# Another order table, and other planned costs, for a four-layer graph-attention kernel

## The chip, the cores and the metric

The kernel runs on one core of one Trainium2 chip. The metric is the device time of one execution in microseconds; the figure for a version is the median of several executions. A core has five engines, each with an instruction queue of its own that it works through strictly in program order: PE (matrix products), DVE (vector), ACT (activations), POOL (general, here small vector work and the issue of accumulating transfers) and SP (issue of plain transfers). The engines wait for each other by semaphores, which the tool chain sets from the data that instructions share. An instruction that has to wait therefore holds up everything behind it in its own queue, also work that could already run.

## What is computed

Sixteen independent graphs (a batch of 16, 1024 nodes, 256 features) pass four layers; all share one 1024 x 1024 adjacency matrix. Before each layer there is a layer norm and a ReLU, and each layer's result is added to its input.

```python
h = jnp.maximum(_layernorm(x, axis=-1), 0.0)
x = x + _L0_gnn_ref(h, adj, L0_gnn_W, L0_gnn_a)      # one-head graph attention, relu
h = jnp.maximum(_layernorm(x, axis=-1), 0.0)
x = x + _L1_gnn_ref(h, adj, L1_gnn_W, L1_gnn_a)      # one-head graph attention, elu
h = jnp.maximum(_layernorm(x, axis=-1), 0.0)
x = x + _L2_gnn_ref(h, adj, ...)                     # 8-head dot attention, norm, feed-forward, norm
h = jnp.maximum(_layernorm(x, axis=-1), 0.0)
x = x + _L3_gnn_ref(h, adj, L3_gnn_W, L3_gnn_a)      # four-head graph attention, elu
```

In a graph-attention layer the weight of node j for node i is the softmax over j of leaky_relu(e_i + e_j) where the adjacency is set. In layer 2 it is the softmax of q k / sqrt(32) where it is set, head by head.

## The kernel before

The work is cut into **stages**, one for each layer and graph (64 of them), and stages of up to four graphs are interleaved. All of it is written down first as 12,154 small operations (`op(...)`): for each an engine, a cost in us, the operations that it comes after, and the buffers that it takes and ends. One operation is a handful of instructions, for example four matrix products.

`play()` then lays the operations out. It calls `forward(rank)`, a list scheduler that keeps a clock for each engine, adds each operation's cost to it, and adds `DELAY[engine]` before a result counts as seen elsewhere. At every step it looks at the operations that could start on an engine, takes those that could start within 0.5 us (`SLACK`) of the earliest, and picks the one of lowest rank. Changes of PE's tile shape are charged by `SWITCH`. The ranks come from a long string, `RANKS`, with three characters for each operation; since it has the right length, it is used and no other ranks are tried. The order in which operations are picked is the order in which instructions are emitted on every engine's queue. So both the string and the costs decide the order, and neither is in the program that runs: they cost no instruction.

The operations that the prediction speaks of, with their lines in the profile:

- **Layers 0 and 1**: eight weight blocks on DVE (p, L1362), then the products `av` on PE (L1379, eight operations of four products for each half of the nodes), whose result in one of two PSUM banks is inverted on DVE (L1396), taken out by ACT (L1402, L1417) and added on DVE (L1407, L1421, L1422).
- **Layer 2**: `scores` on PE (sc, L1597; four heads), two exponentials on ACT (L1611), two mask products on DVE (L1619), `values` on PE (acc, L1628). For each pair of such items a 1,024 KB transfer that adds one tile to the other (pe<-pe) is issued on POOL (L1645), and `totals` on PE (sums, L1658) uses the result. At the end of a half: a copy on ACT (L1668), transposes on PE (L1677), normalisation, feed-forward products `up` and `down` (both L1097), between them a transfer that adds an offset row to y (y<-offsets, issued on POOL, L1733) and another to x. Then DVE adds (L1797), ACT squares the result (L1071), POOL takes the root (L1074, L1075), DVE scales and adds (L1812, L1819).
- **Layer 3**: weight blocks on DVE (L1443) after a transfer of source values (r<-kept, SP), `values` on PE (acc, L1477) and `totals` (sums, L1501).
- **The way into each layer**: squares or statistics, a root, a normalisation on ACT or DVE (L1151, L1135, L1144), eight transposes on PE (tp, L1090), a copy on ACT (hT, L1093), then products (pm, L1097).

A second path through the file, for inputs that break the fast path's assumptions, is compiled and not run here.

PE works with three tile shapes: the whole array, 32 rows by 128 columns (scores) and 128 rows by 32 columns (acc and sums of layers 2 and 3).

Of the kernel before, what the change touches and what calls it, by code (L numbers as in the profile page):

```python
# [28 lines left out]
U8 = mybir.dt.uint8  # L29
# [3 lines left out]
AX = mybir.AxisListType  # L33
PSUM = bass.MemoryType.PSUM

P = 128
# [11 lines left out]
    "$7K#`;$57#};#U[#8d#-f##%###$'v#;a#.U##$#$5#$&$6j#Pq#$(#cE##E#$W#$<#xV##=#%#$Jw#$;##,#$H#$o#+$#Jm#$w#+d##+#%?$1;"  # L48
    "#H)#&R#')#'C#'O#'.#':#'R#'b##f#+###3##r$=O##I##j#*}##H##v#*b#Tz#cL#`U##0##6##C#$I#$G#$T#Gf#$7##5#$F#iA#$_##-#%)"
    "##y#ok##F##|##G##h#$'#`@#*-#$-#*i#`R#S$#WI#$}#%U##4#%x#$[#$Z##z#$E#$i#$2#%p#we#$O#%t#*j#*`#$A##&#$C#)>$&R$<_#vY"  # L50
    "$<6#JZ#%V#)u#)2#$K#(K#(-#wg#%h#&4#&%#&]##x#$Q##u##.#%l#%z#$@##P#$|#''#$a#-m#$]#]<#'?#%:#$D$BL#$j#]:#%7#&Y$H;#&8"
    "#%D$19#$:#AB#%u#&?#}=#&S#%9#%_#',#&A#'-#&q#v_#$P##Y#&B#%i#&w#'g#&`#'7#%n#'I#_p#L=#b##$h#$p##L#$u#$q#$y#%%#$L##W"
    "#%-#%W#%<#%`#'a#'6#&(#%3#%d#&t#cA#%J#&H#A:##R#%[#%k##9#'U#%s##`#,L#'&##S#%g#$4#'`#%B#%v$#8##c#%f#&z#c:#$e$Iu#Xf"
    "$*R#&9#%}#Xg#&:#_/$-O#uE#%G#*g#EY#T8#ui#$c$CA$H8#$n#3%#Tp#%F#2b#%@#${$Ew#&C##b#%M#$f#$0#%H#$z#$%#%/#$l#%4#$M#%N"
    "#%8#%e##(#&I#%+#t<#j?#%,$.f#&M#%.#2?#]0##n#'E#$v#%$#$t#$m#%m#%^#'j#(m#'H#(d#$x#&*#&[#&o#%q##J#']#-@#%P#%1#'Q#vX"
    "#EX#:B#$.#%I##7#$d#%a##_##8#$3#'W#'{#&'#/r#%=#az$KE#$b#'4#L`#$$#b$#0:#_0$*r#R9#$##&m#+q#*$#09#&u$*q$Kt#&1#'>#05"
    "$7h#R8#%0##a#0F#[F#'T#&i#$J#G>#&e#_g#ov#(,#GS#(}$:)#&K#%r#&^#%A#&n#&&#%&#$B$8R#&v$Ks#&j$LG#Fy#'%#JJ#&/#)P#&$$(M"
    "#&p$08#uH#tF#o7#)O#&F#%o#%b#&+#*(##X$9B#&>#%O$9##'|$9Y#DY#$>#'P#'_#'l#(5#)@#'}#?+#%6#(6#Y.#[N#[M#<R#0j#(##%2#q_"
    "#qN$9n#*M##K#&c#&b#'=#$R#1Q##Z##2#o4#$*#($#$?#(/#%R$9p#oM#&V#I8#-2#DZ#Kr#1d#,B#&G#'9#Jq#*q#$8$9v$:_#y7#6?#'f#K="
    "#(s#r:#(r#'*$Bb#_s$%L#([#JM#(<#AL#(I#w_#r5#&E#&P#(%#,_#(*#VI$+d#'c#'q#KL#.-#(f#-V$4l$Je#'r#((#;3#H+#<&#)#$?&#AO"  # L60
    "#ck#(8#&O#vO#83$5F$:^$7.#(.#(C#&g#(J#&=#(R#)K#(V#(l#(U#)0#)%#)|#)D#)S#+2#;7#%w#&a#$)#'1#&_#%*#$`#(7#(X#%y#(y#i*"
    "#&h#u,#re#(_#(W$0=$23$0<#&U$FK#&T#(L#(2#K##(D$/n#)r#0n#(A#(v#(N$0;#)q#(0#)p#0m$8Y#)3#)-#Gq#4f#)x#)E$$A#=Q#G]#'L"
    "#i+#H8#'d$3a#Jy#()#)/#)8#'t#)b#(a$8u#vv##B#)1#)9#D,#)g#,q##A#vo##@#)6#)Y#)7$Ho#)+#QW#uq#),#(@#)d#'F#$N#)*$=##)C"
    "#+k#*:#*s#,g#-r#+0#71#0t#0(#(|#q<#D4#pz#D:#*>#)R$6w#(e#QZ#D(#,.#)G#`-#*T#*9#*a#.j#,1#*B#*H#*l#Dk#LC#*'#-j#*W#'["
    "#u4#*Q#*4#{s#-h#D3#9J#*_#*J#p|#B##La#.8#*v$5.#7I#+4#*[#eE#.D$IK#*u#*U#*S#)h#.>#(P#.<#*X$;}#+B#=B#+R#*h#nE$+q#(O"
    "##]#*f#*]$5?$Ij$M.#+m#+>$5%#u3#+Q#+<$L]#>x#Ig#+l#*V#+=#/'#[p$B@#<;#+^$-|#Y_#+Y#*%$B?#zG#XR#K{#+L#+&#+c$O%#+j#<_"
    "#+i$4}$<>#+u#*y#)_#y($Ai#}A#+g#+]$C,$6m#Wb#L%#,,#M=#aC#{a#+5#rn#,>#C/#+`#+[$Ek#?>#*8#,f$0H##D#)4#)T#*K#+|#jE#+%"
    "#&X#,n$G;#,'#(G#..#e2#+b$7r#?k#Qu#)L#g9#*m#on#nl#.Z#+-#=R#Jt#.'#.]#-x#.H$E4#H@#-U#-a#/_#.G#.P#0.#-]#l;#*x#/V#/L"
    "$(9#.O$OJ$Dr#.I#/f##<#0B#.N#^T#/9#.*#-W#.r#.9#1)#0<#/U#.S$A:#D1#fV#;2#/3#.;#+,#+*$<H#y)#Va$9G#+f#,/$Ah#*<#LD$7-"
    "#,*#VV#T&#,9#-+$?)$Bc#M<#C'#{>#)W#rY#Cn$:i#Cm#,C$-{#T%#,o#,7#/,$7D#4e#+C#,^#,6#/.#+a$:h#)}#,v#aB#['#,V#+M#&W#,N"  # L70
    "#0g#?R#-Q#,d#.,#,;#+)#?Q#-O#0-#(F$Oa#+O#+.#(h#,}#*P#,u$Dz#-$#.0#,Z#l4#-&#,D#+9$7;#-?#,j#(g#-%#]s#,0$/$#+w#m:#,h"
    "#]e#,8#-=$?3#RV#0D#-N#nI$Mt$7v##*$G=#-y#,a#.V#Ht#/4#,M#(`#p9$(y#.J#l<#+1#,W#:a#/b#,e#om#*7#-q#*R#+H$Do#*w#1+#+G"
    "#/z#,l#-u#,z#,|#.R#.$#-(#*/$>o#.a#oP#.:#--#/%#+K#-B#/>#._#-X#.^#o,#.b#.v#Qz#BC#mJ#QP#0h#`=#-G$J{$Kv#(M#&s$5D#.A"
    "#&r#0$#)m#1P#,y$J0#1Z#0+#&-#-w#be#,{#/}#*O#/k#-A#&)#,U#/g#,(#+z#/5#0)#h0#,`#-p#,r#'2#,X#.C#g0#/t#0k#u$#0/#/{#-^"
    "#+_#.{#/6#/K#/Y#/X#1&#*e#.B$,_#]3#_(#oN#(b#0l#VS#)`#)^#*Z#*&#,?$0z#+/#+h#,k#*t#*,#*G#**#*L#(3#8+$8;#*)#+($59$J|"
    "#WB$.g$J_#yG#+e#)n#+:#-;#)o#+3#-e#,O#LX$0E#2J#+D#*A#I3#*z#dg#.=#s,#s-#.w$/X#+E#,J#*C#+7#/+$'I#Tk#A-#)l#+o$6d$#`"
    "#,x#|=#)B#-S#-_#-I#-|#-}#-v#)?#/l#+}##?#0U#S:#^S#0X#2M$(x#-8#.t#.h#9|#-R#mG#ff#.d$CJ#(H#/H#:.#t##/0#/($B;$)K#/#"
    "#[?$=C#[a#-K#/[#.K#.u$7m#,Q$5H#,G#mt#/v#,F#3D$5G#jF$KK$>T#.p#2D#od##>#S;#2E$CI#.q#q^#Kz#.7#0>#//#.E#EF#Sr#0*#hd"
    "#tv#f?#P0#-*#0E#0C#/8#,&#/^#mu$=<#-t#0?#2Y#l&#/J$<;#mA#{f#/o#Ci#-M#8`#1J#3,#29#`D#0L#if#ie#pF#0G#;p#{H#8k#/)#]?"
    "#_<#[z#+;#+Z#+T#+{#30#1*#1i#,R#+N#+U#Do#1;#./#ol#q}#/y#H&#31#qH#-o#)Z#.4#Gk#}x#4K#/T#Yz#0`#0K#15#.[#2o#1j#0H#.&"  # L80
    "$J3#/x#0]#,##+J#/P#/Q$'V#0r#0Z#0z#1?#1$#1F#1R#0[#1/#0f#/$#11#1>#03#5.#1E#1:#2m#1[$N-#1o#0o#@-#(Y#5<#);#b4#1(#aA"
    "#1z#6]#7Y#/1#-c#1Y#^6$JQ#1e#/7#12#1C#Se#2*$;s#@1#H^$*{#0x#-b#0p#9y#1k#?b#/]#1y#(Z#1f$BO$-i#e-#tJ#2&#/&#cO#0S#5;"
    "#1g$1/#2=$Hh#1h#bj#0b$-h$*T$*(#2B$*6$+|#0|$JU#2)#1=$*4#{*#2T$K7#2X#2(#1^#@.#M%#2O#/e#/m#5'#p{#2^#0%#/d#4E#7e$K6"
    "#53#2G$+T$>W#21#1n#/Z#S)#-k#A+#0^#1B#-1#T.#nV#6W#2[#>%$@p#2Z#2'$Iw#58#1`#[-#1s#2C#,t#]b$Iv#,:#4O#46#M'#26#/?#nW"
    "#(k#pq#2$#2:#2Q#oX#^v$$m#.1#3/#Hk#>$$>V#0M#>B#1m#3;#.F#2A#3C#3>#2_#3M#4D#3T#/G#3Q#42#3U$-]#3N#8n#3v#9f#3P#8j#5q"
    "#?I#44#)i#6t##[#2@#`<#4]#(?$1m#5`#4J#*N#4T#33#OG#*Y#7.#:*#,K#50#L1$C4#t'#U+#*E#R*#7)#1D#zf#zI$-u#1I#/A#8.#5X$Cp"
    "#3B#wq#/E#kJ#37#3i#2|$26#4;#7U#35#7^#:>#59$;,#5x#4x#7=#7L#3L#1q#B9#[w#qy$5Z#2h#2N#oL#WY#OF#[v#43$Bg#4s#3##1x#B'"
    "#o6#D7#,5#2d#2f#mK$'$#K,$#o#3.#3t$?6#1|#07#Ju$OZ#?P#3K#^<#2e#bA#32#mM$'G$EU#3[#4r#2z#25#b_#3A$-?#3R#HV#23#1T#3G"
    "$=J#2W#2##+@#3s#L9#4>#3+$M,#3W#2n#3e#2y#3?$*f#3Z$+R#3]#e5#47#$,#5a#3'#-i#34#+?#1l#3^#17#9S#3f#3<#3u#3w$Mg##l#TB"
    "#2x$1Q#3x#4j#41#4&#2w#J6#4-$7G#4I#40#3g#3@#4Z#3m#70#F|$4s#GO#4<#4,$;Q#B>#7/#6O#4|#BQ#4m#<C#uo$Ld#5_$C8#4?#1<#4N"  # L90
    "#24#3d#4P$.*#5C#6s#3=#4l#5Q$8E#5>#80#3O#-F#69#4k#3}#-E#5O#Be$I|#'D$5/#^V#3S#s`#2l#5h#94#1G#76$?T#5W$Ec#7N#1p#5L"
    "#5y#Bm#By#9W#9k#$1#Br#1,#6a#Bl#5V$Eg#6v##o#7?#6w#f@#Av##e#uz#/i#3|#0J#0O$O$#0T#1t#5s#0P#7##2F#V3#0R#Mm$IW#2{#61"
    "#[4#2]#[0$?H$?A$?R#Bs#F{#6(#6P#6'#zP#Mz#6&#4Q#4=#4C#4y$03#7@#(x#4U#oZ#3($A-#5]#1S#l##4B#tj$+P#T2#5%#51$;Y#60#4F"
    "#X%#s@#5)#5B#36#4:$60#Y=#5o#49#5b#1W$1h#nw#5{#9##78#X9#aw#4%#6j#5z#6n#R,$FF#Qw#5H#5S#7R#2R#fi#6|$6$#r0#5R#5j#Bf"
    "$7+#4##7m#77$IX#5n#6-#6z#7(#7A#W=#6b#}t#6Y#75#hw#W2#hv#yy#7$##^#6Q$Bi#Nj#Vr#o5$*x#Dd$3z#5/#5,#4{#5i#0Y#F7#62#5$"
    "#3*#.T#7z#8O#6d#3c#-s#.W#6i#6u#5##5^#.s#.6#6Z#XQ#6m#6x#r)#7B#O:#7u#2S#79#8U#7i#:?#{N#9O#9h#%K#7g#7V#@9#nv#7|#%]"
    "#8G#7[#6^#8;#85#7k#8-#8S#8D#8B#7v#68#9,#M;$9,#TE#8b#?a#8a#;##8H#9&$>)#<q#8J#_q#Lm$'3#HE#,$#7C#2p$4.#7'#k8#nm#7D"
    "##'#Y0#7G#5v#Em#8R$JF#8&#5g#3V#6o#6{#7%#8N#6D#7a#7t#7P#7K#4^#6G#7T#6;$)%#Y@$El#4w#7-#k`#7d#7x#:8$JE#4*#4v#7J$Kh"
    "#9$#l=#5U#8X$1j#7;#7+#7{#4t#3I#4i#:;#SW#G(#45#4h#@]#@[#Ks#:x#9H#;x#9'#x-#x]#;w#:v$<7#7_#Z&#87#d1$@?#g+#d6#6`#8'"
    "#:P#nX#'e#mW$F<#<6#8s#9Z#<p$>-#-4#86$Eh#<)#6N#98#cl#-g#cq#Ln#Ft#;r#9B#0I#9l#8F#9=#9:#:r#:)#9i#9%#2.#2-$N}#5k#74"  # L100
    "#'m#'z#_M#8E#:o#9?#9M$ER#K7$/m#5[#@W$0,#9D#9[#cp#8e$Ej#/R#F.$,u#9g#9A#&k#:l$,t#<##@_#G&#/D$({#'<#;}#xH#9Y#?p#';"
    "#9R#:I#9d#2r#:s#6K#Ab#8K#&2#:H#8u#;o#I>#x'#9Q#:t#93$#a$#n#8P$/p#;V#mX$+G$B0#95#7p#;U$=h$HX#9E#Fe#;s#:e#9z#9<$IZ"
    "#Cj$3S#84#:4#:9#xo#:(#yc#9{#@^#[A#:y#9K#&3#IB#8w#x.#:`##;#8v#I@#7M#um#:k#cB#Z,#;5#9}$16$,Z#QY#=$#;M#6e#Qb#ns$K-"
    "$,Y#:d#8$$Ki#dk#;=#9>#:=#J:#89#?'#9t#6)#:<#jC#9;#em#;@$DX#<A#;C#9u#:c#4[#;N#el#;1#6I#<8#4n$DP#:}#;k#AX#uT#;P#5J"
# [515 lines left out]
def fast_path(tc, bad, x, adj, l0_w, l0_a, l1_w, l1_a, w_qkv, ln1_g, ln1_b, ln2_g, ln2_b, w1, b1, w2, b2, l3_w, l3_a, out):  # L620
# [13 lines left out]
    with ctx:  # L634
# [128 lines left out]

        ops = []
        PE, DVE, ACT, POOL, SP, QUEUE = range(6)

        DELAY = (0.2, 0.12, 0.14, 0.06, 2.0, 1.4)
        ITSELF = 0.04  # L770

        SWITCH = {None: 0.2, 132: 0.21, 32: 0.125}


        BEFORE_END = 0.1
# [1268 lines left out]
```

## Time and profile before

| what | value |
|---|---|
| median of 3 runs | 4212.4 us (4209.66 to 4214.54) |
| the profiled execution's own time | 4213.85 us |
| its span | 4212.1 us |
| PE busy | 4093.9 us, 97% |
| DVE busy | 3170.0 us, 75% |
| ACT busy | 2322.9 us, 55% |
| POOL busy | 1169.6 us, 28% |
| DMA queue q0 (the POOL-issued transfers) | 302.01 MB, 36.5% of 16 engines' span |
| granted PE clock | 0.994 of full speed |

The profiled execution took 1.4 us more than the median; its span is 1.8 us shorter than its own time. A group line names source line, engine, operation, output and input tiles, then busy time, the mean of one, and the engine's idle time before it with what ended it. A busy PE in this profile can contain waits, because the ends of overlapping products are modelled; the starts are recorded.

### The profile page before, as it was taken

How to read it: one execution, taken by the hardware profiler on the slowest of the kernel's cores; microseconds unless marked ns; L12 is line 12 of the kernel's file. 1: busy time of each engine (PE TensorE's matmuls, PEld its weight loads, DVE VectorE, ACT ScalarE, POOL GpSimd, SP SyncE). 2: the span in 40 equal slices, each digit the busy share in tenths (PEclk: the TensorE clock that was granted, in tenths of full speed). 3: DMA queues.
4: the chain of work that ended last, by engine and by line, in shares of the span. 5: the costliest groups of instructions: out<-in, count | busy, mean ns of one | idle time of the engine just before them, and what ended most of it. 6: DMA issues, size and time to landing. Idle time of an engine off the chain costs nothing.

```text
span 4212.1 us, 67534 instructions
## 1 busy us (share of the span) xinstructions
PE 4093.9 (97%) x25993; PEld 2160.5 (51%) x25993; DVE 3170.0 (75%) x5964; ACT 2322.9 (55%) x4235; POOL 1169.6 (28%) x2025
## 2 busy tenths in 40 slices
PE   8999999999999999999999999999999999999997
PEld 7735255553555536455364654546545465564433
DVE  7577867778677786777867778776787877859697
ACT  5564645636456364564646646465463745666452
POOL 2322231412314123141331423223132241423131
PEclk9999999999999999999999999999999999999999
DMA  3171814518145181451815518164271733636361
GB/s 124 34 158 35 176 45 96 111 49 170 39 99 107 51 170 36 112 108 37 170 38 116 113 35 162 41 135 91 53 151 33 159 67 79 121 82 132 72 135 47
DMA packets 106826, 398.96 MB, mean 95 GB/s; under 512 B 11528, under 2 KB 47744, under 8 KB 73728
## 3 DMA queue, kind: packets, MB, share of 16 engines
q0 software_dynamic: 46080, 302.01, 36.5%
q1 hardware_dynamic: 60000, 92.03, 6.7%
q8 instruction: 206, 3.38, 0.3%
q14 instruction: 124, 1.02, 0.1%
q10 hardware_dynamic: 416, 0.52, 0.0%
HBM read 107.87 MB, written 18.21 MB: 30 GB/s over the span
## 4 chain that ended last, share of the span: by engine, by line
PE 74%; DMA 7%; DVE 6%; issue 6%; ACT 4%; POOL 2%; SPq 0%; POOLq 0%; ACTq 0%; DVEq 0%
PE pm L1097 19%; PE av L1379 18%; PE acc L1477 10%; PE sc L1597 8%; PE acc L1628 6%; DMA pe<-pe 5%; PE sums L1501 5%; PE sums L1658 3%; PE tp L1090 3%; DVE pe L1619 2%; DMA y<-offsets 2%; ACT pe L1611 1%; DVE y L1797 1%; ACT pm L1071 1%; PE tpv L1540 1%
## 5 line engine op out<-in xcount | busy, mean ns | idle before, releaser
L1619 DVE TENSOR_TENSOR pe<-pe,mask 128x1024 f32<-128x1024 f32 x1024 | 1200.6, 1219 | 208.7 <-ACT pe L1611 205.1
L1611 ACT ACTIVATE pe<-sc 128x1024 f32<-128x1024 f32 x1024 | 998.0, 1022 | 321.0 <-PE sc L1597 228.0
L1379 PE MATMUL av<-v,p 128*128 128x257 f32 x4096 | 956.7, 384 | 21.7 <-ACT o L1402 10.7
L1379 PEld LDWEIGHTS av<-v,p 128*128 128x128 f32 x4096 | 764.9, 191 | 210.9 <-issue 60.8
L1443 DVE SCALAR_TENSOR_TENSOR p<-r,e,mask 128x1024 f32<-128x1024 f32 x512 | 623.0, 1274 | 114.6 <-DMA r<-kept 98.0
L1597 PE MATMUL sc<-qT,kT 32*128 32x512 f32 x4096 | 620.9, 642 | 2.7 <-ACT pe L1611 1.5
L1628 PE MATMUL acc<-pe,v 128*32 128x512 f32 x4096 | 538.3, 604 | 1.3 <-DVE pe L1619 0.6
L1645 POOL DMA_DIRECT2D pe<-pe x256 | 224.7, 878 | 992.5 <-PE acc L1628 628.7
L1074 POOL TENSOR_SCALAR rstd<-stats 128x1 f32<-128x1 f32 x512 | 159.0, 311 | 1153.4 <-ACT xn L1071 739.8
L1477 PE MATMUL acc<-p,v 128*32 128x512 f32 x4096 | 463.0, 593 | 0.0
L1597 PEld LDWEIGHTS sc<-qT,kT 32*128 32x128 f32 x4096 | 189.8, 183 | 379.4 <-issue 174.7
L1097 PE MATMUL pm<-l_wx,hT 128*128 128x259 f32 (+1 forms) x1536 | 369.5, 389 | 8.1 <-ACT hT L1093 5.2
L1362 DVE SCALAR_TENSOR_TENSOR p<-r,e,mask 128x512 f32<-128x512 f32 x512 | 349.1, 743 | 24.8 <-DMA r<-kept 19.1
L1075 POOL TENSOR_TENSOR rstd<-rstd,minus_half 128x1 f32<-128x1 f32 x512 | 331.6, 648 | 42.7
L1097 PEld LDWEIGHTS pm<-l_wx,hT 128*128 128x128 f32 x1536 | 287.4, 191 | 79.1 <-ACT hT L1093 20.7
L1658 PE MATMUL sums<-pe,pick 128*32 128x512 f32 x2048 | 269.5, 603 | 28.6 <-DMA pe<-pe 27.8
L1477 PEld LDWEIGHTS acc<-p,v 128*32 128x32 f32 x4096 | 131.1, 110 | 296.1 <-issue 282.1
L1628 PEld LDWEIGHTS acc<-pe,v 128*32 128x32 f32 x4096 | 94.2, 108 | 339.8 <-issue 206.4
L1051 POOL TENSOR_SCALAR rstd<-stats 128x1 f32<-128x1 f32 x256 | 131.9, 515 | 454.5 <-DVE stats L1048 450.8
L1501 PE MATMUL sums<-p,e 128*32 128x512 f32 x2048 | 242.3, 593 | 0.0
L1097 PE MATMUL pm<-hT,qkv_sb 128*128 128x512 f32 x512 | 228.6, 593 | 2.6 <-ACT hT L1093 2.3
L1052 POOL TENSOR_TENSOR rstd<-rstd,minus_half 128x1 f32<-128x1 f32 x256 | 207.8, 812 | 21.3
(122 smaller groups left out, 4133.0 us busy)
## 6 DMA issues: line engine op xcount, KB each, us to landing
pe<-pe POOLq DMA_DIRECT2D x256, 1024.0 KB, 8.7
r<-kept SPq DMA_DIRECT2D x64, 512.0 KB
x<-in_x_dram SPq DMA_DIRECT2D x32, 512.0 KB
x<-offsets POOLq DMA_DIRECT2D x32, 512.0 KB, 5.5
y<-offsets POOLq DMA_DIRECT2D x32, 512.0 KB, 5.8
out_dram<-x SPq DMA_DIRECT2D x64, 256.0 KB
r<-kept SPq DMA_DIRECT2D x62, 256.0 KB
edges<-in_adj_dram SPq DMA_DIRECT2D x8, 512.0 KB
```

Source lines behind the costliest of these rows:

```text
L1075: nc.gpsimd.tensor_tensor(rh.t, rh.t, minus_half, ALU.pow)
L1097: nc.tensor.matmul(dst, lhsT=lhsT[:, k, :], rhs=rhs[:, k, :], start=(k == 0), stop=(k == KC - 1))
L1362: nc.vector.scalar_tensor_tensor(ph.t[:, j % each, :], rh.t, s.e[:, j, H + h : H + h + 1], mask[:, j, cols], ALU.max, ALU.mult)
L1379: nc.tensor.matmul(avh.t[:, : s.hs + 1], lhsT=phs[part].t[:, j % each, i * P : (i + 1) * P], rhs=s.v[:, j, h, :], start=(j == 0), stop=(j ...
L1443: nc.vector.scalar_tensor_tensor(ph.t[:, hh, :], s.rh[hp].t[:, hh, :], s.e[:, j, col : col + 1], mask[:, j, :], ALU.max, ALU.mult)
L1477: nc.tensor.matmul(acc[n].t[(2 * hh + part) * W : (2 * hh + part + 1) * W, :], lhsT=s.v[:, jj, h, part * W : (part + 1) * W], rhs=p, start ...
L1501: both(lambda jj, n, hh, h, p: nc.tensor.matmul(sums.t[(2 * n + hh) * W : (2 * n + hh + 1) * W, 0, :], lhsT=s.e[:, jj, 2 * H + h : 2 * H + ...
L1597: nc.tensor.matmul(scs[pair].t[:, hh, :], lhsT=s.kh.t[r0 : r0 + D2, g, j * P : (j + 1) * P], rhs=s.qh.t[r0 : r0 + D2, g, cols], start=True ...
L1611: lambda pair=pair: nc.scalar.activation(part(pair), scs[pair].t, AF.Exp, scale=SCALE2),
L1619: lambda pair=pair: nc.vector.tensor_tensor(part(pair), part(pair), masks(), ALU.mult), [ex], tiles=True,
L1628: nc.tensor.matmul(head(acc, i), lhsT=s.v[:, j, g * QUAD + i, :D2], rhs=ph.t[:, i, :], start=(j == 0), stop=(j == NT - 1))
L1658: nc.tensor.matmul(head(sums, i), lhsT=pick[:, g, :], rhs=th.t[:, i, :], start=first, stop=last)
```

## The change

Two things are changed, and no operation, buffer or instruction is added or removed.

First, all 335 lines of `RANKS` are replaced. Second, planned costs of small operations and one delay are replaced, most by larger values:

```diff
-        DELAY = (0.2, 0.12, 0.14, 0.06, 2.0, 1.4)
+        DELAY = (0.2, 0.12, 0.14, 0.06, 2.0, 1.8)
...
-            m_op = op(DVE, 0.54, rank, stats, after, takes=[mh, rh, *takes])
-            r_op = op(POOL, 1.1, rank + 0.6, root, [m_op], ends=[mh])
+            m_op = op(DVE, 0.55, rank, stats, after, takes=[mh, rh, *takes])
+            r_op = op(POOL, 1.4, rank + 0.6, root, [m_op], ends=[mh])
...
-            q_op = op(ACT, 0.49, rank + 0.4, square, after, takes=[rh, *takes], ends=ends)
-            r_op = op(POOL, 1.4 if shift else 1.15, rank + 1.0, root, [q_op], ends=[mh])
+            q_op = op(ACT, 0.52, rank + 0.4, square, after, takes=[rh, *takes], ends=ends)
+            r_op = op(POOL, 1.5 if shift else 1.2, rank + 1.0, root, [q_op], ends=[mh])
...
-                add = op(DVE, 0.46, rank + 0.9, add_one, [o], takes=[mh], ends=[oh], tiles=True)
+                add = op(DVE, 0.54, rank + 0.9, add_one, [o], takes=[mh], ends=[oh], tiles=True)
...
-                add = op(DVE, 0.95, rank + 1.3, add_both, [o], takes=[mh], ends=[eh, oh], tiles=True)
+                add = op(DVE, 1.08, rank + 1.3, add_both, [o], takes=[mh], ends=[eh, oh], tiles=True)
...
-                c = op(DVE, 0.8, rank + 3.7 + 4.0 * u, add, [a, shifted[0]], takes=mhs)
+                c = op(DVE, 1.05, rank + 3.7 + 4.0 * u, add, [a, shifted[0]], takes=mhs)
...
-                        DVE, 0.5, at + 3.0, add_scaled, [centred, r_op, shifted[1]], takes=[nh], ends=[s.yh, rh], tiles=True
+                        DVE, 0.64, at + 3.0, add_scaled, [centred, r_op, shifted[1]], takes=[nh], ends=[s.yh, rh], tiles=True
```

In the same way the normalisations on ACT (L1135, L1151) go from 0.4 to 0.49, the ReLU (L1402) from 0.37 to 0.39, the exponential of three columns (L1233) from 0.2 to 0.08, `see` (L1273) from 0.35 to 0.2 and the transpose of the sources (L1294) from 0.2 to 0.11. The last entry of `DELAY` belongs to transfers issued by POOL. Together they give another order on all five queues: row by row, PE's sequence goes from 3,411 rows of equal neighbouring instructions to 3,403, DVE's from 4,650 to 4,680, ACT's from 2,677 to 2,647, POOL's from 1,890 to 1,895 and SP's from 172 to 171, with differences in nearly every stage.

## The prediction

> **What bounds the kernel now.** First the page's busy times, then the costliest groups.
>
> ```profile
> span 4212.1 us, 67534 instructions
> ...
> PE 4093.9 (97%) x25993; PEld 2160.5 (51%) x25993; DVE 3170.0 (75%) x5964; ACT 2322.9 (55%) x4235; POOL 1169.6 (28%) x2025
> ...
> L1379 PE MATMUL av<-v,p 128*128 128x257 f32 x4096 | 956.7, 384 | 21.7 <-ACT o L1402 10.7
> ...
> L1597 PE MATMUL sc<-qT,kT 32*128 32x512 f32 x4096 | 620.9, 642 | 2.7 <-ACT pe L1611 1.5
> ```
>
> PE is the bound, and by its row an order of work could gain at most 4212.1 - 4093.9 = 118 us. [...] The trace lets me price it by starts instead. A product of 257 columns has a mean of 384 ns in the row, but the next one starts 0.216 us later (median of 3,804 pairs). So I took for each planned PE operation the time from its first start to the next operation's first start, and as its usual spacing the value that 85% of its kind reach or exceed, kept apart by whether the tile shape changes. In us:
>
> - av 512 x 1.739 = 890; scores 512 x 0.962 = 493; layer 2's acc 512 x 0.882 = 452; layer 3's acc 128 x 3.433 = 439; the two sums 256 x 0.858 + 128 x 1.716 = 439
> - attention projections 192 x 1.750 = 336; layer 2's q, k, v, up, down 64 x 3.432 + 32 x 3.453 + 32 x 3.452 + 32 x 3.431 = 550; all transposes and small ones 234
> - 1,352 changes of tile shape, 145 in all (a next start 0.308 instead of 0.216 after av, 0.523 instead of 0.409 out of the 32-column shape)
>
> That is 3,978. Before PE's first product lie 7.6 us, after its last operation starts 17.3. [...]
>
> The waits of PE say who ends last (total, times, longest):
>
> ```profile
> PE sums L1658 <- DMA pe<-pe: 27.8, 35, 2.5
> PE pm L1097 <- ACT hT L1093: 15.0, 18, 1.4
> PE tp L1090 <- ACT xn L1151: 13.3, 9, 7.6
> PE av L1379 <- ACT o L1402: 10.7, 9, 5.6
> PE tps L1677 <- ACT sums_sb L1668: 7.4, 5, 5.7
> ```
>
> The 5.7 us wait is typical of the long ones. The timeline around it:
>
> ```profile
> 516.39 1.21 POOL L1733 DMA_DIRECT2D y<-offsets  x1
> ...
> 524.71 3.62 PE L1097 MATMUL pm<-w_sb,hT 128*128 128x256 f32 x16
> ...
> 533.59 0.42 DVE L1797 SCALAR_TENSOR_TENSOR y<-y,pm 128x256 f32<-128x256 f32 x1 [5.47 <-DMA y<-offsets]
> ...
> 535.68 0.48 ACT L1071 ACTIVATE pm<-y,stats 128x256 f32<-128x256 f32 x1 [8.25 <-DVE y L1797]
> ...
> 539.79 0.56 ACT L1668 COPY sums_sb<-sums 128x512 f32<-128x512 f32 x1
> ...
> 540.41 1.11 PE L1677 MATMUL tps<-ident,sums_sb 128*128 128x128 f32 x4 [5.69 <-ACT sums_sb L1668]
> ```
>
> The offset transfer, behind two 1,024 KB ones issued at 511.10 and 515.86, lands 17 us after its issue. DVE's add waits; ACT's squares of it stand ahead of the copy in ACT's queue; PE waits for the copy. No engine is short of time here; the order in a queue was made as if the add came earlier.
>
> **The change part by part.** No instruction goes or comes, so every effect is one of order. "Lead" below is PE work, by the usual spacings, that stands between two PE operations in an order.
>
> *PE's own work.* Counted in the new order, tile shapes change 1,352 times, as before. By kind: 397 to 399 (32-column to scores), 389 to 383 back, 169 to 174 and 161 to 158 (whole array into and out of 32-column), 114 to 111 and 122 to 127 (into and out of scores). At 0.09 to 0.11 us each this is under 1 us: the sum is 3978.7 for 3979.2. **0 us.**
>
> *Scores waiting for exponentials.* 74.5 us of stall. In the old order 174 scores have under 1 us of PE work since the last scores ended and lose 0.257 us each; in the new order 174. The next class (1.5 to 2 us, 0.111 each) goes 178 to 170. Classes priced by the old means give 75.3. **+1 us**; DVE's and ACT's time for them is unchanged and no order can spread them without other work.
>
> *Products right behind their transposes.* With a lead under 0.2 us the copy on ACT is exposed, 1.63 us on average. 12 cases become 10; all classes 34.8 to 31.8. **-3 us.**
>
> *Sums behind the 1,024 KB transfer* (DELAY 1.4 to 1.8). The lead from the first of the pair's acc to its sums has a median of 9.9 us, now 10.4; below 8.5 us stand 31 of 256, now 10, at 0.24 us each. All classes: 24.6 to 20.8, **-4 us**. [...]
>
> ```profile
> pe<-pe POOLq DMA_DIRECT2D x256, 1024.0 KB, 8.7
> ...
> y<-offsets POOLq DMA_DIRECT2D x32, 512.0 KB, 5.8
> ```
>
> [...] The rows say 8.7 and 5.8 to landing, and up to 17.1 for the offset, since they queue. I take the rows: -4.
>
> *av's banks, up and down, the other transposes.* By the same classes -1.4, -1.2 and, for transposes at the way in and at the ends of halves, +2.2. **0 us.**
>
> *Long stalls.* For the stalls over 0.3 us (138 us) I followed the trace from the late PE operation back, through waits and through queue neighbours, to the PE operation on which the chain hung, and compared the lead between the two in both orders. It grew for stalls of 55.6 us, shrank for 33.7, stayed within 0.1 us for 48.7 (for the rest no PE operation was found). Each grown lead taken off its stall, each shrunk one added: 138 to 122, **-16 us**. About 8 of it is the end of the run, where little other work is left:
>
> ```profile
> 4122.80 0.44 PE L1090 MATMUL tp<-ident,xn 128*128 128x128 f32 x2 [1.78 <-ACT xn L1151]
> ...
> 4127.70 6.28 PE L1097 MATMUL pm<-l_wx,hT 128*128 128x268 f32 x16 [1.11 <-ACT hT L1093]
> ```
>
> The last transposes come 10.4 us after the last `down` instead of 5.3, the last `down` 1.3 us after `up` instead of 0, a scores at 4063 us 11.2 instead of 7.5 us behind its root: of 13 us stalls there I expect 5 to be left. In the stall at 540 us the lead from `down` to the transposes grows only from 9.7 to 10.9, and the copy still stands behind the squares; what helps is that the first of the two transfers is now triggered 2.9 us earlier against the offset's.
>
> *DVE, ACT, POOL, SP.* The raised costs (L1407, L1797, L1819, L1151, L1074) move about 0.1 to 0.25 us per operation in the plan, nothing on the chip. Their idle time (1042 us on DVE) covers any reshuffle that keeps the leads. DVE's wait for r<-kept (98.0 us) feeds layer 3's acc, whose lead from the sources' transpose goes from 14.9 to 18.2 us at its short end; PE lost 0.5 us there: **0**. SP's and POOL's other rows only follow.
>
> The sum: +1 - 3 - 4 + 0 - 16 = **-22 us**. The classes count new stalls with old ones, the chains only old ones; the overlap (products behind transposes, 3 us at most) I leave, since stalls under 0.3 us behind DVE and ACT queues were given nothing. On the profiled execution's 4213.85 this gives 4191.9; the median shown lies 1.4 lower, so **4190 us**. Bounds: by the classes alone -6 (4206); if half of the stalls over 1 us go, -48 (4164); all of them, -97, is the most I can imagine.
>
> **The rivals.**
>
> - *Long stalls mostly vanish.* They come from queue positions that assumed too early adds, and the assumed costs are now near the rows. For: seven of the fifteen longest have grown leads. Against: of nine copies and exponentials on ACT that I followed, seven still stand behind the same squares. Half of 97: 4164 us.
> - *Shuffling only.* What is taken from one stall comes back in another, as with the shrunk leads of 33.7 us: 4212 us.
> - *Slower: offsets behind two transfers.* Where both 1,024 KB transfers are triggered within about 3 us before the offset's or after it, the trace has the add 18 to 20 us (lead plus wait) after the transposes that trigger it. In the new order this pattern appears for the last graph (triggers 3.0 before and 1.0 after, lead only 10.3 us) and with a cut lead for another (16.7 to 13.2). Waits of 8 and 4 us on DVE, passed on to PE as the 5.5 us wait was, cost 12; it decides if the -16 doesn't come and at least one more half shows the pattern: 4212 + 12 = 4224 us. Against: in six of the nine halves where the add was late by over 0.8 us, the lead has grown.
>
> **How the numbers follow.** The forecast (4176 to 4203) 0.62, long stalls vanish 0.23, shuffling 0.09, slower 0.06. About 0.2% (8 us) can be told from no change by a measurement of this kernel. Faster by more: 0.62 + 0.23 = 0.85; within: 0.09; slower: 0.06. The range reaches down to 4156, past the half, and up to 4208, past the class sum.
>
> **What would show it.** Right: PE's changes of tile shape cost the same, stalls by starts fall from 210 to about 188, the sums' wait for pe<-pe falls from 27.8 towards 20, few waits of tps, av and tp over 4 us, the end with under 2 us before the last transposes. Wrong: new waits over 4 us behind ACT's squares in the middle, or a y<-offsets wait on the last graph's add; the scores' stall moving by more than 5 us would break the class prices.

## The result, and the profile after

| | before | after |
|---|---|---|
| median | 4213.97 us (4209.66 to 4217.3, 6 runs) | 4194.98 us (4190.34 to 4199.96, 6 runs) |
| ratio | | 0.9956, 95% interval 0.9944 to 0.9969 |
| span of the profiled execution | 4212.1 us | 4188.6 us |
| stalls of PE, summed by starts | 209.9 us | 185.7 us |
| of them, stalls over 1 us | 96.9 us in 52 | 80.7 us in 46 |

The change made the kernel 19.0 us faster by the medians; the two profiled executions lie 23.5 us apart, because the one of after was the fastest of its six. "Stall" is meant as in the prediction: from a PE operation's first start to the next one's, less the usual spacing of its kind. The 210 and 97 us from which the prediction's bounds and signs start are the last two rows of the table: the span of 4212.1 us less 3978 of usual spacings and 25 at the two ends leaves 209, summed one by one 209.9. PE's busy row leaves only 118 us (4212.1 - 4093.9), so 90 us of stalls stand inside that row, most of all behind the starts of scores.

The page of after, busy times and the two groups shown of before:

```profile
span 4188.6 us, 67542 instructions
...
PE 4085.4 (98%) x25993; PEld 2158.0 (52%) x25993; DVE 3174.7 (76%) x5964; ACT 2319.6 (55%) x4235; POOL 1207.9 (29%) x2025
...
L1379 PE MATMUL av<-v,p 128*128 128x257 f32 x4096 | 951.9, 382 | 10.2 <-ACT o L1402 6.0
...
L1597 PE MATMUL sc<-qT,kT 32*128 32x512 f32 x4096 | 619.8, 640 | 5.1 <-ACT pm L1071 4.3
```

The instruction counts of the five engines are the same; the total is 8 higher, all of it wait instructions that carry no work. PE's busy time fell by 8.5 us although its work is the same, so this row holds waits or time at a lower clock. The `av` products lost half of their idle time (21.7 to 10.2 us); the scores gained a wait that they didn't have, 4.3 us behind an ACT square.

The waits of PE in after (total, times, longest):

```profile
PE sums L1658 <- DMA pe<-pe: 20.6, 29, 1.9
PE pm L1097 <- ACT hT L1093: 14.2, 16, 1.4
...
PE acc L1628 <- DVE pe L1619: 6.1, 7, 3.8
PE av L1379 <- ACT o L1402: 6.0, 9, 1.3
PE tps L1677 <- ACT sums_sb L1668: 5.7, 5, 3.4
PE tp L1090 <- ACT pe L1611: 4.8, 2, 4.6
PE sc L1597 <- ACT pm L1071: 4.3, 1, 4.3
```

Two waits over 5 us that before had, `av` behind o and tps behind sums_sb, are down to 1.3 and 3.4 at the longest. In return there are three new single waits of about 4 us (3.8, 4.6 and 4.3). Where the stalls went, in us:

| stall before | before | after |
|---|---|---|
| scores | 74.5 | 71.8 |
| av | 38.8 | 27.5 |
| products right behind their transposes | 34.8 | 24.0 |
| layer 2's sums | 24.6 | 16.5 |
| tps and tpo (end of a half) | 12.6 | 10.1 |
| acc | 4.9 | 7.8 |
| way-in transposes | 5.7 | 8.3 |
| up | 1.1 | 7.5 |

This booking is the prediction's. Its row of the scores holds every stall that follows the start of a scores operation, also one that ends only at the next operation. Split at the last product of each operation, by the same starts, the waits inside scores are 37.9 us before and 36.7 after, those ahead of scores 1.3 and 3.2, and those ahead of layer 2's sums, whatever stands in front of them, 30.3 and 21.9: 14.0 and 12.0 us of these stand in the table's row of the scores.

The rise of up is likewise a stall of 5.7 us that sits inside the acc in front of it:

```profile
3818.10 0.75 DVE L1362 SCALAR_TENSOR_TENSOR p<-r,e,mask 128x512 f32<-128x512 f32 x1 [5.12 <-DMA r<-kept]
3818.77 1.22 DVE L1619 TENSOR_TENSOR pe<-pe,mask 128x1024 f32<-128x1024 f32 x1
...
3820.04 1.92 PE L1628 MATMUL acc<-pe,v 128*32 128x512 f32 x4 [3.83 <-DVE pe L1619]
...
3821.89 5.59 PE L1097 MATMUL pm<-hT,w_sb 128*128 128x512 f32 x8
```

DVE waits 5.1 us for the source values (r<-kept) of a graph-attention weight block. The mask product stands behind that block in DVE's queue, and PE's acc waits for the mask product.

The largest new stall, 6.3 us by starts, is that of scores in the last graph's layer 2: 4.4 us before their first product and 1.9 inside them. The timeline of after around it:

```profile
4022.08 0.86 POOL L1645 DMA_DIRECT2D pe<-pe  x1 [3.61 <-issue]
...
4022.62 1.21 POOL L1733 DMA_DIRECT2D y<-offsets  x1
...
4026.12 3.72 PE L1097 MATMUL pm<-w_sb,hT 128*128 128x256 f32 x16
...
4034.18 0.42 DVE L1797 SCALAR_TENSOR_TENSOR y<-y,pm 128x256 f32<-128x256 f32 x1 [4.54 <-DMA y<-offsets]
...
4036.27 0.48 ACT L1071 ACTIVATE pm<-y,stats 128x256 f32<-128x256 f32 x1 [8.11 <-DVE y L1797]
...
4038.68 1.92 ACT L1611 ACTIVATE pe<-sc 128x1024 f32<-128x1024 f32 x2
...
4038.82 2.99 PE L1597 MATMUL sc<-qT,kT 32*128 32x512 f32 x8 [4.35 <-ACT pm L1071]
```

It reads like the stall at 540 us in before. `down` (the pm row) ends by 4029.8, but the offset was issued behind a 1,024 KB transfer and lands 11.5 us after its issue (the offsets' median in after is 6.9). DVE's add starts at 4034.18, four squares on ACT come 2 us behind it, and the exponential that would free PE's bank for the next scores stands behind these squares. This is the third rival of the prediction, in the place that it named, but inside a run that is faster all the same.

At some points of the order both versions have issued the same operations. Between such points, read from the starts of the same PE operations in the two traces, the time fell by 33.5 us up to operation 7,714 of 12,154, with two stretches inside it that lost 3.5 and 4.8 us. It rose by 2.5 us from there to operation 11,618, and by 9.2 us from there to 11,896, the stretch with the new stall; the rest gave back 2.9. PE's first product came 1.1 us later. So the question was: does each stretch own its gain or loss, and which resource carries it?

### The profile page after: what moved, and what is told of

Same layout as the page of the kernel before. It is cut to its first block, busy times and chain, and to the rows that moved or that the text cites. A ratio compares the mean times of both kernels' runs of the same rounds, so it can differ in the third digit from the quotient of the medians.

```text
span 4188.6 us, 67542 instructions
## 1 busy us (share of the span) xinstructions
PE 4085.4 (98%) x25993; PEld 2158.0 (52%) x25993; DVE 3174.7 (76%) x5964; ACT 2319.6 (55%) x4235; POOL 1207.9 (29%) x2025
## 3 DMA queue, kind: packets, MB, share of 16 engines
q0 software_dynamic: 46080, 302.01, 36.7%
## 5 line engine op out<-in xcount | busy, mean ns | idle before, releaser
L1379 PE MATMUL av<-v,p 128*128 128x257 f32 x4096 | 951.9, 382 | 10.2 <-ACT o L1402 6.0
L1074 POOL TENSOR_SCALAR rstd<-stats 128x1 f32<-128x1 f32 x512 | 166.6, 325 | 1157.9 <-ACT xn L1071 695.6
L1362 DVE SCALAR_TENSOR_TENSOR p<-r,e,mask 128x512 f32<-128x512 f32 x512 | 347.7, 742 | 30.5 <-DMA r<-kept 27.1
L1075 POOL TENSOR_TENSOR rstd<-rstd,minus_half 128x1 f32<-128x1 f32 x512 | 331.9, 648 | 42.7
L1658 PE MATMUL sums<-pe,pick 128*32 128x512 f32 x2048 | 268.5, 600 | 21.1 <-DMA pe<-pe 20.6
L1051 POOL TENSOR_SCALAR rstd<-stats 128x1 f32<-128x1 f32 x256 | 138.5, 541 | 441.7 <-DVE stats L1048 438.7
L1052 POOL TENSOR_TENSOR rstd<-rstd,minus_half 128x1 f32<-128x1 f32 x256 | 221.8, 866 | 21.3
```

Source lines behind the costliest of these rows:

```text
L1075: nc.gpsimd.tensor_tensor(rh.t, rh.t, minus_half, ALU.pow)
L1362: nc.vector.scalar_tensor_tensor(ph.t[:, j % each, :], rh.t, s.e[:, j, H + h : H + h + 1], mask[:, j, cols], ALU.max, ALU.mult)
L1379: nc.tensor.matmul(avh.t[:, : s.hs + 1], lhsT=phs[part].t[:, j % each, i * P : (i + 1) * P], rhs=s.v[:, j, h, :], start=(j == 0), stop=(j ...
L1658: nc.tensor.matmul(head(sums, i), lhsT=pick[:, g, :], rhs=th.t[:, i, :], start=first, stop=last)
```

## The experiments

Medians in us; each ratio is to the kernel before in runs on the same chip. Its median was 4211.2 to 4215.1 us on the chips used, so a difference between the medians of two rows can contain a few us of the chips. The last column is the granted clock missing in the profiled execution, the sum of (1 - clock) x 4 us over windows of 4 us, without the 5 to 8 us behind the last products.

| run | median | ratio, 95% interval | PE stalls | missing clock |
|---|---|---|---|---|
| before | 4213.97 | 1 | 209.9 | 20.4 |
| after | 4194.98 | 0.9956 (0.9944 to 0.9969) | 185.7 | 13.7 |
| table_only | 4427.29 | 1.0508 (1.049 to 1.0525) | 419.2 | 68 |
| costs_only | 4399.32 | 1.0449 (1.0426 to 1.0472) | 390.7 | 75 |
| before_no_yoff | 4189.25 | 0.9946 (0.9929 to 0.9963) | 188.3 | 8.5 |
| after_no_yoff | 4173.11 | 0.9910 (0.9893 to 0.9927) | 171.0 | 10.2 |
| splice_new_old | 4184.7 | 0.9941 (0.9924 to 0.9958) | | 10.2 |
| splice_old_new | 4219.84 | 1.0021 (1.0014 to 1.0028) | | 22 |
| splice_12 | 4172.89 | 0.9911 (0.9894 to 0.9927) | | 6.8 |
| end_old | 4178.99 | 0.9917 (0.9904 to 0.9931) | 172.8 | 8.5 |
| offset_first | 4187.22 | 0.9935 (0.9921 to 0.9948) | 176.1 | 6.8 |
| before_no_gather | 4146.09 | 0.9839 (0.9826 to 0.9853) | 144.8 | 3.4 |
| after_no_gather | 4131.22 | 0.9803 (0.979 to 0.9816) | 130.5 | 0 |
| kept_busy | 4191.27 | 0.9948 (0.9934 to 0.9961) | | 13.6 |

### Is it the string of ranks or the costs?

Each half of the change alone, put into the kernel before:

```diff
 RANKS = (
-    "$7K#`;$57#};#U[#8d#-f##%###$'v#;a#.U##$#$5#$&$6j#Pq#$(#cE##E#$W#$<#xV##=#%#$Jw#$;##,#$H#$o#+$#Jm#$w#+d##+#%?$1;"
+    "#pO##/#29$4?#/<#._#28$Km#-d#9d#1K#/V#Yt#%>#$h$?-#+7#$u##6#(,#&-#$p#%O##O$As#;U#%U##.#$R#&L#,|$3z#':#-2#_.#'G#XJ"
...
```

> The new RANKS string with the old costs and DELAY; nothing else changed, the same instructions. Theory A (the string carries the gain, the costs only serve the search): as the changed kernel, about 4195 us, ratio 0.995 to 0.997. Theory B (string and costs belong together, because the scheduler that lays the operations out reads both; with the old costs 1,109 of PE's 2,747 operations get another predecessor than in the changed kernel): the gain is lost, 4205 to 4230 us, ratio 0.998 to 1.004.

and the costs and the delay of the new kernel with the old string:

```diff
-        DELAY = (0.2, 0.12, 0.14, 0.06, 2.0, 1.4)
+        DELAY = (0.2, 0.12, 0.14, 0.06, 2.0, 1.8)
...
```

> The old RANKS string with the new costs and DELAY. Theory A: as the kernel before, 4212 us, ratio 1.000. Theory B: also an order that nobody searched for, 928 of PE's operations get another predecessor; no better than before, 4210 to 4235 us. If the truer costs alone help (theory C: the scheduler places waits better with them), 4200 us or less.

Both are 4 to 5% slower than either kernel. Theory B has the direction, but its range ended at 4230 and 4235 us. With other costs the same string gives another order. Of PE's 2,747 operations 1,352 have another predecessor in after than in before; with the string alone 1,109 differ from after, with the costs alone 928 differ from before. In costs_only the waits of PE show what that order costs:

```profile
PE acc L1477 <- DVE p L1443: 32.0, 15, 6.3
PE sums L1658 <- DMA pe<-pe: 28.8, 34, 3.0
PE pm L1097 <- ACT hT L1093: 19.0, 22, 1.2
PE tps L1677 <- ACT sums_sb L1668: 18.5, 5, 11.8
```

Layer 3's acc waits 32 us for weight blocks; that wait is not among those shown of before or after. So the gain can't be split into "better string" and "truer costs": string and costs belong together.

### Do the offsets' transfers carry the gain?

Both orders without the 32 transfers y<-offsets, so that the offset row isn't added to y:

```diff
             def start():
+                if which == 0:
+                    return
                 nc.gpsimd.dma_start(out=(s.y, xs[s.b])[which][:, ts, :], in_=offsets[which], accum_op=ALU.add)
```

> The kernel before without its 32 y<-offsets transfers (the offset rows of the layer-2 feed-forward are not added); order of everything else unchanged. It removes the cause of DVE's late adds at L1797. Theory D (the change gained because the pile-ups behind these late adds went): the kernel before falls by 20 to 30 us, to about 4188, and the changed kernel without them by much less (under 10), so that the two end within 5 us. Rival E (the pile-ups behind the offsets cost both orders alike and the gain is elsewhere): both fall by the same amount within 5 us.

> The changed kernel without its 32 y<-offsets transfers (offset rows not added). Theory D: falls by under 10 us from 4195. Rival E: falls by as much as the kernel before does, 15 to 25 us, to about 4175. In both, the 6.3 us stall of scores at 4039 us behind ACT's squares must go, which alone is 4 to 6 us.

The fall is 25 and 22 us, alike within the intervals: the offsets are worth over 20 us in either order. Without them the orders still lie 16.1 of 19.0 us apart. That the gain lies mainly in offsets that wait less is refuted, although DVE does wait less for them. Before and after:

```profile
DVE y L1797 <- DMA y<-offsets: 17.7, 5, 6.2
...
DVE y L1797 <- DMA y<-offsets: 10.2, 4, 4.5
```

### Do the stretches own their stalls?

For these kernels the order of the operations and the buffer place of each were written out, so that stretches of the two orders can be joined where both have issued the same operations. In `play()`:

```diff
-                best = forward([(x * 90 + y) * 90 + z for x, y, z in zip(digits[::3], digits[1::3], digits[2::3])])
...
-            for _, _, o in best[1]:
+            digits = [DIGITS.index(c) for c in ORDER]
+            places = iter(DIGITS.index(c) for c in HELD_IN)
+            for x, y, z in zip(digits[::3], digits[1::3], digits[2::3]):
+                o = ops[(x * 90 + y) * 90 + z]
```

First the new order up to operation 7,714 and the old one behind it, and the reverse; then twelve stretches, each from the faster of the two traces.

> Order written out instead of scheduled: the new order for the first 7,714 operations, the old order for the rest (both orders hold the same operations up to there, about 2642 us in the new one's trace). Up to this point the new order's trace is 41 us ahead, and from there to the end it loses 17.6 us. Theory F (a stretch's stalls belong to the stretch's order, so stretches add up): 4195 - 17.6 = about 4177 us, ratio 0.991 to 0.993. Rival G (what one stretch saves, another gives back, whichever order follows, since late transfers and queues are handed over): no better than the changed kernel, 4190 to 4200 us. My forecast's step 'the end gains 8 us' says the opposite of F: the new end is the better one, so this splice would be some 8 us slower than the changed kernel, 4203.

> The reverse: the old order for the first 7,714 operations, the new one for the rest. Theory F: 4213 + 17.6 = about 4231 us, ratio 1.003 to 1.006. Rival G: about 4205 to 4213. If the new end is the better one (my forecast's step): about 4205 us.

> Twelve stretches, each in that of the two orders whose trace was faster there (choices by one profile each, so part of it is chance). The traces add up to 4172 - 38 = 4134 us to the last product against 4172 for the changed kernel. Theory F: about 4160 us after some regression, ratio 0.986 to 0.989, faster than both kernels. Rival G: 4185 us or more.

One correction to these expectations: their figures of 17.6, 38 and 41 us counted the 8.7 us before PE's first product as if they belonged to a stretch. The right sums are 8.8 us lost behind operation 7,714 and 29.5 us for the twelve stretches. Against them stand 10.3 us gained (4194.98 to 4184.7) and 5.9 lost (4213.97 to 4219.84). Taken against the 4211.17 of the runs beside them these are 7.5 and 8.7, and the twelve stretches gained 22 of 29.5 by the medians, 19 against the runs beside. The interval of the twelve lies clear of after's, that of the first join does not. So stretches do own most of their stalls. What was picked by one execution's luck needn't come again, which may be one reason why not all of the 29.5 came; it was not tested.

The same for the stretch with the new stall alone, operations 11,618 to 11,896 in the old order:

> The changed order with the old order in one stretch alone, operations 11,618 to 11,896 in issue order (the last graph's second layer from about 3,955 to 4,052 us), where the changed kernel needs 9.2 us more than the kernel before. Theory F (a stretch takes its stalls with it): 4195 - 9 = 4186, ratio 0.9934, span about 4179.5. Rival I (the loss in this stretch is only moved: the stretch behind it, 4.9 us shorter in the changed kernel, is shorter because it was left more slack, and gives 4 to 5 us back): 4190 to 4191, ratio 0.9945.

4178.99 us is 16 us under after by the medians and 12.9 by the profiled spans, more than either side expected. By the starts of the same PE operations in both traces, 1.7 us of lead were there before the stretch began (same order of work up to there), 8.5 came in it and 3.1 in the 25 us behind it. The stretch's loss was real, and no stretch behind it took it back.

### One transfer moved

Which instruction made that loss? In the changed order one POOL instruction is moved, the y<-offsets of this stall ahead of the 1,024 KB transfer it stood behind. (The expectation calls it the last one; it is that of the last graph's first half, and one more follows at 4,086.7 us.) In issue order:

```diff
+POOL L1733 y<-offsets
 POOL L1645 pe<-pe
-POOL L1733 y<-offsets
```

> The changed order with one POOL instruction moved: in the last graph's second layer the last y<-offsets is issued before the 1,024 KB pe<-pe transfer that stands ahead of it, not after it. Nothing else differs. In the changed kernel this offset took 11.5 us to land, DVE's add sat idle 4.5 us until it, ACT's squares started that much late, and TensorE stood 6.3 us before the scores behind them. Theory G (the wait of the third rival of the prediction is real and is paid in full): the offset lands about 4 us earlier, the stall before these scores falls from 6.3 to under 2 us, and the time is 4190 to 4191, span about 4184.5; the ratio to the kernel before 0.9945. Theory H (the wait is hidden: what stands after the scores is late for another reason, or the displaced transfer makes its totals late): 4195, ratio 0.9956, and a stall of 3 to 5 us turns up before sums or products within the next 30 us.

The timeline of this kernel (its lines are 18 higher than those of after):

```profile
4017.26 0.87 POOL L1751 DMA_DIRECT2D y<-offsets  x1 [1.34 <-PE tp L1108]
4019.52 0.85 POOL L1663 DMA_DIRECT2D pe<-pe  x1 [1.39 <-issue]
...
4027.31 0.42 DVE L1815 SCALAR_TENSOR_TENSOR y<-y,pm 128x256 f32<-128x256 f32 x1 [0.24 <-PE pm L1115]
...
4029.40 0.48 ACT L1089 ACTIVATE pm<-y,stats 128x256 f32<-128x256 f32 x1 [3.80 <-DVE y L1815]
...
4031.96 2.04 PE L1615 MATMUL sc<-qT,kT 32*128 32x512 f32 x8
```

The offset is issued right behind the transposes that it has to wait for, lands 9.2 us later, and DVE now waits 0.24 us, for the product, in place of 4.54 for the transfer. The stall before the scores is gone from the list of those over 1.7 us. The median is 7.8 us lower, the span 9.7. Of these 9.7, 5.8 were won here, by the starts of the same operations ahead of and behind this place; the rest came in places where the order is the same. The intervals of the two ratios just touch, so the case rests on the trace: the wait for the offset and the stall behind it are gone. Theory G holds; it had set 4 to 5 us.

### What the 1,024 KB transfers cost

Both orders without them, so that the totals are taken from one tile of each pair alone:

```diff
             def gather():
-                nc.gpsimd.dma_start(
-                    out=th.t.rearrange("p i q -> p (i q)"), in_=ph.t.rearrange("p i q -> p (i q)"), accum_op=ALU.add
-                )
+                return
```

> The kernel before without the 256 transfers of 1,024 KB that add one key block's exponentials to another's: the totals are taken from one block of each pair alone, so that the softmax's denominators hold half of the terms. The 24.6 us of stalls before totals, all said to wait for these transfers, should go, and the offsets' transfers, which share POOL's queue with them, should land sooner. Theory J (the totals' stalls are a cost of their own): 4214 - 24.6 = 4189, and 5 us lower if the offsets' waits shrink too. Rival K (TensorE then waits for the exponentials and masks, which are the next to be late): a fall of under 10 us, 4204 or more.

> The same in the changed order; the totals' stalls there are 16.5 us. Theory J: 4195 - 16.5 = 4178.5, again up to 5 us lower through the offsets, and the two orders 11 us apart in place of 19: the leads of the totals are 8 us of the gain. Rival K: a fall of under 7 us, and the two orders still 17 to 20 us apart.

Both theories fell short: 68 and 64 us, not 25 to 30 and 17 to 22. One reason is the booking: the 24.6 and 16.5 us left out the gaps of sums that stand right behind scores. Split at each operation's last product, the stalls ahead of sums fell by 36 us in the old order and by 27 in the new, until none was left, and those inside scores by 6 and 4. DVE's wait for the offsets, 17.7 and 10.2 us, is gone as well: on the queue that they shared with the 1,024 KB transfers, they now land 5.3 us after their issue, where 5.8 and 6.9 were usual. So part of the offsets' price is in the 68 and 64. And the granted clock that is missing falls from 20.4 to 3.4 us and from 13.7 to nothing; at the 1.0 to 1.3 us for each 1.7 that the last experiment reads from its trace, an estimate of this part is 10 to 13 and 8 to 10 us.

For the scores there is a view that the prediction did not read, the waits of ACT. The exponential's row in before's list of groups by line has the idle time and its three largest releasers at its end:

```profile
L1611 ACT ACTIVATE pe<-sc 128x1024 f32<-128x1024 f32 x1024 | 998.0, 1022 | 321.0 <-PE sc L1597 228.0 <-DMA pe<-pe 69.0 <-DVE pe L1619 11.5
```

The same row of the old order without the transfers:

```profile
L1611 ACT ACTIVATE pe<-sc 128x1024 f32<-128x1024 f32 x1024 | 997.4, 1023 | 279.0 <-PE sc L1597 263.3 <-PE sums L1656 3.4 <-ACT pe L1611 0.3
```

The exponential writes into one of eleven large buffers, and the program gives back the tile that a transfer adds only when the transfer has landed. ACT stood 69.0 us waiting for that; in after it is 58.3:

```profile
ACT pe L1611 <- DMA pe<-pe: 58.3, 52, 2.6
```

So the transfer was late in three places: for the sums that read its result, for the exponential that wants its source, and for the offsets behind it in the queue. ACT's idle time fell by only 42 of the 69 us, since it then waits longer for scores, and the waits inside PE's scores fell by 6. What each place is worth in the time was not measured apart.

The two orders lie 14.9 us apart without these transfers (19.0 with them), between J's 11 and K's 17. In the table's booking the orders' difference ahead of sums shrinks from 8.1 to 1.3 us, and the stalls before the projections of the graph-attention layers hardly move (21.3 against 9.4 us with the transfers, 19.4 against 9.1 without). That part of the gain, about 10 us, doesn't hang on these transfers.

### The clock behind a stall

The window view of after around the new stall (PE busy, granted clock, DMA share, GB/s):

```profile
4032.00:4036.00 4.00, 2.48 (x24) 1.00 0.36 73
4036.00:4040.00 4.00, 1.18 (x6) 0.67 0.00 0
4040.00:4044.00 4.00, 4.00 (x20) 0.50 0.97 197
4044.00:4048.00 4.00, 4.00 (x32) 0.98 0.50 100
```

After some 4 us with nothing to do, PE goes on at half clock for 6.8 us, and has work in 5 of them. The windows of before around its stall at 540 us read 0.80, 0.50 and 0.85. In all, before misses 20.4 us of clock outside the run's end and after 13.7, both close to multiples of 1.7. Is that a price, or does it hide in the waits? Matmuls with zero weights were laid behind operations ahead of three stalls:

```diff
+            def idle(number, into, held):
+                for k in range({3812: 14, 11884: 18, 8372: 7}.get(number, 0)):
+                    nc.tensor.matmul(
+                        head(into, k % QUAD), lhsT=pick[:, KC, :], rhs=held.t[:, k % QUAD, :], start=False, stop=False
+                    )
```

> The changed kernel with 39 more matmuls with zero weights, which add nothing: 14, 7 and 18 of 128x512 laid behind the values or totals that stand right ahead of three of its stalls (4.7 us at 1,276, 1.9 at 2,839 and 6.3 at 4,039). At the 0.214 us that these matmuls take, they fill 3.0, 1.5 and 3.9 us in which TensorE stood still. Nothing waits for less: the scores, transposes and values behind them still come when their inputs do. In the changed kernel the granted clock went to half behind each of these stalls, for 3.4 us (1,276), 3.4 us (2,836), and 6.8 us (4,036), and TensorE had work in about 12 of these 13.6 us. Theory L (the half clock is a price of its own, paid on top of the stall): the clock stays at 1.00 in these three places and the span falls by about 6 us, to 4182 to 4183, the time to 4189, ratio 0.9942. Rival M (the half clock is hidden, because the operations behind a stall wait for other engines anyway, or the stall alone is what costs): 4194 to 4197, ratio 0.9956 to 0.9961, with the clock at 1.00.

The windows of this run at the three places:

```profile
1272.00:1276.00 4.00, 3.46 (x32) 1.00 0.38 76
1276.00:1280.00 4.00, 2.86 (x24) 1.00 0.16 33
2836.00:2840.00 4.00, 2.24 (x22) 1.00 1.00 205
2840.00:2844.00 4.00, 4.00 (x26) 1.00 0.51 104
4036.00:4040.00 4.00, 4.00 (x27) 1.00 1.00 160
4040.00:4044.00 4.00, 4.00 (x41) 1.00 0.38 74
```

The clock stays at 1.00 in all three. From the end of each stall to some 10 to 30 us later, the same operations catch up on after by 0.8, 1.2 and 4.2 us, together the 6 of theory L. But the median fell by only 3.7 us (against the kernel before in the runs beside it the gain is 20.1 us where after has 19.0), and the intervals of the two ratios overlap, so by the time it isn't settled. One reason can be seen in the same profile, in places where the program is unchanged:

```profile
472.00:476.00 4.00, 4.00 (x24) 0.61 1.00 213
496.00:500.00 4.00, 3.62 (x20) 0.59 0.90 182
1040.00:1044.00 4.00, 2.19 (x11) 0.86 0.02 4
1044.00:1048.00 4.00, 4.00 (x17) 0.71 0.00 0
```

In the profiled execution of after these four windows read 1.00, with the same instructions. In this one they cost 1.9 us (the first two together) and 1.3 us, read from the starts of the same operations before and behind. So by these traces 3.4 us at half clock, 1.7 us of missing clock, cost 1.0 to 1.3 us here, and whether a stall of about 2 us (1.9, 2.3 and 1.6 in after, by the starts of the products ahead of these three places) brings them differed between these two executions.

## Why the prediction was right

Forecast 4190 us, -22 on the profiled execution; measured 4194.98, -19.0 by the medians and -23.5 by the spans. The sum was right, its parts less so, and that the total agrees is in part luck: the forecast added 6 us of small classes to 16 of long stalls, while in the measurement the stalls over 0.3 us alone fell by 22.4 of the 24.2 us. The two steps were two cuts through the same stalls, and the long stalls gave more than was priced.

- **PE's own work, 0.** Right: 1,352 changes of tile shape in both, usual spacings 3978.3 and 3977.9 us.
- **Scores, +1.** -2.7 in the same booking. All 58 us of stall that follow a scores' start were taken for waits inside for a bank; 38 are, and 14 are gaps ahead of the sums behind them. Those gaps fell by 2.0. The scores' own waits, inside and ahead of them, went from 39.2 to 39.9 us, as forecast.
- **Products behind transposes, -3.** 34.8 to 24.0, -10.8. The lead classes missed most of it. 4.4 us of it are two stalls at the end (4.0 and 2.0 before, 1.6 and none after) that were counted under the long ones too: more overlap than the 3 us at most that the prediction allowed.
- **Sums, -4.** -8.1, and -8.4 with the gaps behind scores. Right in sign, half in size; why the lead alone gave too little was not followed (the transfers' median to landing is no shorter, 8.8 us for 8.7). Pricing the transfer by its row (8.7 us to landing) is borne out: without the transfers 36 and 27 us of stalls ahead of sums go.
- **av, up, down, transposes, 0.** Right as a sum (-2), wrong in its parts: av -11.3 and tps -2.5, against up +6.4, acc +2.9 and tp +2.6. One stall of 5.7 us, the one inside an acc behind r<-kept, makes nearly all of up's rise.
- **Long stalls, -16.** All stalls over 0.3 us, another cut through the same stalls, fell from 145.7 to 123.3, -22.4. Of this step the part "about 8 of it is the end of the run" is the one that failed. In the last 100 us before the last operation's start the stalls did fall from 10.6 to 4.8. But in the stretch just ahead, with the late offset in the last graph's layer 2, 9.2 us were lost. From 3,900 us on there were 23.4 us of stalls before and 28.2 after. The chains followed old stalls back; a new one can't be seen that way. What made up for it was the first 60% of the run, worth 33.5 us with everything in it. Which places in the queues carry these was not tested one by one; by the table it is `av`, products behind transposes and sums.
- **DVE, ACT, POOL, SP, 0.** As busy times right, within 5 us on DVE and ACT; POOL's is 38 us higher. One of its root steps (L1052) took 5.2 us where those around it took 0.57 to 1.4, and behind it stands the new wait of 4.6 us of the transposes at 1,276 us. It ran while DVE did four mask products without a break (1,269.6 to 1,274.2); that this is the cause was not tested. As queues they decided most of the waits. That idle time on DVE "covers any reshuffle" failed: r<-kept was weighed for layer 3 alone, while DVE's wait for it ahead of layers 0 and 1 (L1362) rose from 19.1 to 27.1 us, and one of these waits became the 5.7 us stall of PE.

Of the rivals, "long stalls mostly vanish" did not come (96.9 to 80.7). "Shuffling" is half true: stalls of 4 to 6 us were lost and as large ones came, but the balance wasn't nil. "Offsets behind two transfers" came in the named place at about 6 us where 8 on DVE were expected, and with 5.8 us shown by one moved instruction. It was set against the forecast as an alternative, when it was a term to be subtracted from it: its own price of 12 us, weighed with its chance, would have been a line of the sum. The change eased this fault, DVE's wait for offsets fell from 17.7 to 10.2 us, but 4.5 of the 10.2 are new, in the last graph.

The signs for wrong thus appeared (a wait over 4 us behind ACT's squares, an offset wait of the last graph) together with the signs for right (stalls 185.7 for 188, sums' wait 20.6 for 20). They were signs for single terms, not for the total.

Two versions with the same work beat both kernels clear of the intervals: twelve joined stretches at 4172.89 us and the old end in the new order at 4178.99. The new order with the old one behind operation 7,714 (4184.7) and the one moved transfer (4187.22) lie below after too, with intervals that touch its own. The gain of the change could be had without its loss.

## What to carry to other kernels

When a whole order is exchanged, price old stalls and new ones apart: follow each transfer that stands behind a larger one in its queue to the instruction that reads it, in the new order too, and put what you find into the sum. Read the waits of the engines that feed the bound engine as well, with all their releasers; here a late transfer held up whoever read its result (27.8 us of PE's waits in before), whoever wanted its source buffer (69.0 of ACT's) and the transfer behind it (17.7 of DVE's for the offsets). Before stalls are priced by kind, split each at the last product of its operation, so that a wait is booked to the operation that waits. Where two orders pass through the same points, their stretches can be timed and joined, and the best of both is a better kernel than either.

## What was not expected of the hardware

By these traces a stall can cost more than its length: with the clock kept at 1.00, the operations behind three stalls caught up by 0.8, 1.2 and 4.2 us. In the profiles of before and after the granted clock fell to 0.50 behind most PE stalls of 2 us and more (by the starts of the products, without the run's first 10 us and its end: 7 of 8 in before, 5 of 6 in after), 2.4 to 4.6 us after the stall began. Ahead of the run's end there were nine such stretches in before and six in after, six and four of them of 3.4 us, three and two of 6.8, which makes the 20.4 and 13.7 us of missing clock. Of the 23.5 us between the two profiled spans, the 6.7 us of missing clock are an upper bound for the clock's part; at 1.0 to 1.3 us for each 1.7 missing, an estimate of it is 4 to 5 us.

A stall's length alone did not decide it. In before the half clock at 2,296 us came behind a stall of 2.2 us, while one of 2.8 us at 1,571 us brought none. One order of instructions met half clock at 472, 496 and 1,040 us in one execution (0.61, 0.59 and 0.86 in the windows there) and not in another (1.00). What else decides it these runs don't show. In all, 20.4 of 4212 us of clock were missing in before, 0.5%, which is small but about as large as the change that was measured.
